# STU's projection by disjoint column segments, each with its own sum of mixed matrices, in a fused convolution, attention and STU kernel

## Chip, cores and metric

The kernel runs on one core of a Trainium2 chip. The metric is the device time of one execution in microseconds (us). Before the change it is 6336.3 us, the median of three runs (6332.32 to 6337.62). The profile is of one further execution, with a span of 6345.8 us and a mean granted TensorE clock of 0.921 of full speed.

## What is computed

The reference has two layers on x of shape (4 images, 48, 48, 128), all in fp32. The first is a two-dimensional selective scan (four directions, 256 channels, 16 states) with a depthwise convolution ahead of it and a gate and a projection behind it. The second works on 2304 tokens an image: softmax attention of the normalised tokens with themselves, and then an STU (spectral transform unit), which is the part that the change touches:

```python
def _stu(u, sigma, phi, Mu, Mpp, Mpm):
    # U_plus:  16 causal convolutions of u with the filters phi[:, k]
    # U_minus: the same of u * (-1)^t, times (-1)^t
    out  = einsum('btkd,k,kde->bte', U_plus,  sigma ** 0.25, Mpp)
    out += einsum('btkd,k,kde->bte', U_minus, sigma ** 0.25, Mpm)
    for i in range(3):                       # the three-tap part
        out += einsum('btd,de->bte', shifted(u, i), Mu[i])
    return out

for i, frac in enumerate((1, 2, 4, 8)):      # four "experts" on shorter and shorter heads
    xi = x[:, :T // frac]
    outs.append(zero_padded(_stu(xi, sigma, phi, M_u[i], M_phi_plus[i], M_phi_minus[i])))
out = sum(outs[i] * weights[i])
```

Every convolution is causal, so its value at a token doesn't depend on where the sequence is cut. All four experts therefore need the same convolutions and differ only in the matrices behind them and in how many tokens they cover: all 2304, the first 1152, the first 576 and the first 288. A token among the first 288 needs the weighted sum of four matrices, one among the last 1152 that of a single one.

## The kernel before

**Stages.** The program is written in a fixed order for each engine[...]. For each image there is a stage of scans (24 chunks of 384 positions, 8 units each, so 192 units) and a stage of attention, in which the next image's prologue is interleaved. TensorE's spare time in the scans takes other work: in image 0's scans the mixing of the STU matrices (`mixture`), in the scans of images 1 to 3 the STU of the image before (`stu`). The STU of image 3 runs alone at the end. `scans` deals this work out by columns: after each quarter of a unit, `more` draws pieces of it until its share of the total columns is done. The totals are `MIX_COLS` and `STU_COLS`, beside `CHUNK_COLS` = 6144 columns a chunk for the scans' own matmuls.

**STU.** Tokens are laid out in four phases of 576 positions, and positions in five blocks (`BLOCKS`), of 128, 128, 128, 128 and 64 positions. An item is a block and one of the 16 filters, 80 items an image. For each item six convolutions (`conv`, L990) multiply Toeplitz tiles `tt`, loaded by overlapping rows from `fd`, with the stationary tokens; ScalarE and VectorE combine them into `U` (eight groups of the block's positions). `project` (L1056) then multiplies U with two matrices a sign, and sums over the 16 filters in one PSUM bank. It runs one item late: after the third convolution of the next item. `ar` (L1046) opens the bank with the three-tap part. `fetch` (L960) keeps four `tt` buffers filled, `fetch_G` (L971) loads the item's mixed matrices `G` into one of two buffers right after the item's first convolution, and `begin` (L1029) loads those of the three-tap part, `mue`, once a block. All these loads go through the SyncE queue.

**Which matrix where.** The four experts end at positions 576, 288, 144 and 72 of a phase. So block 0 changes its sum at 72, block 1 at 16 columns (144 - 128), block 2 at 32 (288 - 256), and blocks 3 and 4 don't change. The fourth entry of `BLOCKS`, `extra`, is that column. Before, the matmuls overlap: the sum of the experts that reach over the whole block is applied to all of its w columns, and the matrix of the one expert that ends inside it to its first `extra` columns, added in PSUM. The scratch tensors `gd` and `mud` hold six matrices each for this, and the third entry, `place`, says where the pair of the block begins.

**Mixing.** `mixture` runs over the 16 filters k. It loads `M` (four experts, two signs; L829) through the SyncE queue, lets ScalarE build diagonal matrices `W` (L833, L834), and multiplies (L847): for each sign q one PSUM tile (j = 1) with running sums, made by broadcasting one expert's matrix over several slots, and one (j = 0) with single matrices. `keep_` copies a tile to SBUF on ScalarE (L822), one group late, and after the second tile stores the pair to `gd` through the SyncE queue (L824). `weights` does the same for the three-tap matrices, on VectorE, in the first image's prologue.

Of the kernel before, what the change touches and what calls it, by code (L numbers as in the profile page):

```python
# [8 lines left out]
F32 = mybir.dt.float32  # L9
AF = mybir.ActivationFunctionType  # L10
ALU = mybir.AluOpType
# [4 lines left out]
P = 128  # L16
B, H, W, C = 4, 48, 48, 128
# [8 lines left out]
KF = 16  # L26
NF = 4
# [6 lines left out]
SLOT = 2 * (LF + 1)  # L34


BLOCKS = [(0, 128, 0, 72), (128, 256, 2, 16), (256, 384, 4, 32), (384, 512, 5, 0), (512, 576, 5, 0)]
SHIFT = 55.0


# [14 lines left out]
def hybrid_kernel(ctx: ExitStack, tc: tile.TileContext, a: dict, out: bass.AP):  # L55
# [3 lines left out]
    nc = tc.nc  # L59
# [3 lines left out]
    res = ctx.enter_context(tc.tile_pool(name="res", bufs=1, space=DRAM))  # L63
# [72 lines left out]
    zs = res.tile([NH, P, L], F32, name="zd")  # L136
    td = res.tile([L, C], F32, name="td")
    ud = res.tile([P, 4, 1 + LF], F32, name="ud")
    gd = res.tile([KF, P, 2, 2 * NF - 2, C], F32, name="gd")
    mud = res.tile([P, 2 * NF - 2, 3, C], F32, name="mud")  # L140
    fd = res.tile([KF, 3, 2, LF + P], F32, name="fd")
    xdd = [[res.tile([P, CS], F32, name=f"xdd{k}_{c}") for c in range(L // CS)] for k in range(2)]

# [597 lines left out]

    MIX_COLS = KF * 2 * 2 * (6 + 3) * C

    ws = wp.tile([P, KF, NF], F32, name="ws")

    def weights(one):

        def load(name, shape, src):
            t = one.tile(shape, F32, name=name)
            nc.scalar.dma_start(t, src)
            return t

        lg = load("lg", [P, NF], a["log_weights"].partition_broadcast(P))
        gu = load("gu", [P, NF], a["gumbel"].partition_broadcast(P))
        sg = load("sg", [P, KF], a["sigma"].partition_broadcast(P))
        ph = load("ph", [KF, 2, 2, LF + P + 1], a["phi"])  # L760
        mu = load("mu", [P, NF, 3, C], a["M_u"].rearrange("i j d e -> d i j e"))
        for i in range(6):
            yield
        hard, wts = [one.tile([P, NF], F32, name=n) for n in ("hard", "wts")]
        m = one.tile([P, 2], F32, name="m")

        nc.vector.tensor_add(lg, lg, gu)
        nc.vector.tensor_reduce(m[:, 0:1], lg, AX.X, ALU.max)
        nc.vector.tensor_scalar(lg, lg, m[:, 0:1], None, ALU.subtract)
        nc.scalar.activation(lg, lg, AF.Exp)  # L770
        yield

        fc = one.tile([KF, 3, 2, LF + P], F32, name="fc")
        n = LF + P
        nc.vector.tensor_copy(fc[:, 0], ph[:, :, 0, :n])
        yield
        nc.vector.tensor_sub(fc[:, 1], ph[:, :, 1, 1:], ph[:, :, 0, :n])
        yield
        nc.vector.tensor_sub(fc[:, 2], ph[:, :, 1, :n], ph[:, :, 0, :n])
        nc.scalar.dma_start(fd, fc)  # L780
        yield
        nc.vector.tensor_reduce(m[:, 0:1], lg, AX.X, ALU.add)
        nc.vector.reciprocal(m[:, 0:1], m[:, 0:1])
        nc.vector.tensor_scalar_mul(lg, lg, m[:, 0:1])
        nc.vector.tensor_reduce(m[:, 0:1], lg, AX.X, ALU.max)
        nc.vector.tensor_scalar(hard, lg, m[:, 0:1], None, ALU.is_equal)
        nc.vector.memset(m[:, 1:2], 1.0)
        yield
        for i in range(NF):

            nc.vector.tensor_tensor(hard[:, i:i + 1], hard[:, i:i + 1], m[:, 1:2], ALU.mult)
            nc.vector.tensor_tensor(m[:, 1:2], m[:, 1:2], hard[:, i:i + 1], ALU.subtract)
        nc.vector.tensor_sub(wts, hard, lg)
        nc.vector.tensor_add(wts, wts, lg)
        yield

        quarter = one.tile([P, KF], F32, name="quarter")
        nc.vector.memset(quarter, 0.25)
        nc.gpsimd.tensor_tensor(sg, sg, quarter, ALU.pow)
        mum = one.tile([P, 2 * NF - 2, 3, C], F32, name="mum")  # L800
        nc.vector.tensor_scalar_mul(mum[:, 5], mu[:, 0], wts[:, 0:1])
        for i in range(1, NF):
            nc.vector.tensor_scalar_mul(mum[:, 6 - 2 * i], mu[:, i], wts[:, i:i + 1])
            if i < NF - 1:
                nc.vector.tensor_tensor(mum[:, 5 - 2 * i], mum[:, 7 - 2 * i], mum[:, 6 - 2 * i], ALU.add)
            yield
        nc.scalar.dma_start(mud, mum)
        for i in range(NF):
            nc.vector.tensor_scalar_mul(ws[:, :, i], sg, wts[:, i:i + 1])
        zero = one.tile([P, 4, 1], F32, name="zero")  # L810
        nc.vector.memset(zero, 0.0)
        nc.scalar.dma_start(ud[:, :, 0:1], zero)

    def mixture(pool, ps):

        late = []
        banks = [0]

        def keep_(G, p, j, k, q):
            nc.scalar.copy(G[:, :, j], p)  # L822
            if j == 0:
                nc.sync.dma_start(gd[k, :, q], G.rearrange("p s j c -> p (s j) c"))  # L824

        for k in range(KF):
            M = [pool.two.tile([P, NF, C], F32, tag=f"M{j}", name=f"M{j}_{k}") for j in range(2)]
            for t, src in zip(M, ("M_phi_plus", "M_phi_minus")):
                nc.sync.dma_start(t, a[src][:, k].rearrange("i d e -> d i e"))  # L829

            W = pool.two.tile([P, 2, NF, P], F32, tag="W", name=f"W{k}")
            for i in range(NF):
                nc.scalar.activation(W[:, 0, i], ident, AF.Copy, scale=ws[:, k, i:i + 1])  # L833
                nc.scalar.activation(W[:, 1, i], nident, AF.Copy, scale=ws[:, k, i:i + 1])  # L834
            yield 0
            for q in range(2):
                G = pool.two.tile([P, 3, 2, C], F32, tag="Gm", name=f"Gm{k}_{q}")
                for j in (1, 0):
                    p = ps.psc.tile([P, 3, C], F32, tag=("c", "q0", "q1")[banks[0] % 3], name=f"G{k}_{q}_{j}")
                    banks[0] += 1  # L840
                    for i in range(NF):

                        n = NF - 1 - i if j else 1
                        if i == (NF - 1 if j else 0):
                            continue
                        for t in range(2):
                            nc.tensor.matmul(p[:, :n] if j else p[:, NF - 1 - i], W[:, q if t else 0, i],  # L847
                                             M[t][:, i].unsqueeze(1).to_broadcast([P, n, C]) if j else M[t][:, i],
                                             start=(t == 0 and (i == 0 or not j)),
                                             stop=(t == 1 and (i == NF - 2 or not j)))  # L850
                            yield n * C
                    if late:
                        keep_(*late.pop())
                    late.append((G, p, j, k, q))
        keep_(*late.pop())

    def begin_stu(b):
# [6 lines left out]
    def tail(b, J, T, po, pool, ps):  # L864
# [38 lines left out]
        for j in range(4):  # L903
# [5 lines left out]
        nc.sync.dma_start(ud[:, :, 1 + P * J:1 + P * J + k], uT.rearrange("c (j p) -> c j p", j=4))  # L909

    STU_COLS = sum(KF * 12 * sum(hi - max(lo, J * P) for J in range((hi + P - 1) // P))
                   + (2 * KF + 3) * 4 * (hi - lo + extra) + 4 * (hi - lo) for lo, hi, place, extra in BLOCKS)

    def stu(b, pool, ps):

# [15 lines left out]
        tts, Gs, Q, U, now, nxt = {}, {}, {}, {}, {}, [0]  # L931
        late = []
        banks = {}
# [98 lines left out]

        def parts(w, extra):

            return ((w, 1), (extra, 0)) if extra else ((w, 0),)

        def ar(n):

            (lo, hi, place, extra), k = items[n]
            w = hi - lo  # L1040
            p = ps.psp.tile([P, 512], F32, tag="p", name=f"pr{b}_{n}")
            now["p"] = p = p[:, :4 * w].rearrange("p (f r m) -> p f r m", f=2, r=2)
            for i, (v, x) in enumerate(parts(w, extra)):
                for j in range(3):
                    src = now["x"][:, 2 - j:6 - j].rearrange("p (r f) m -> p f r m", f=2)
                    nc.tensor.matmul(p[:, :, :, :v], now["mu"][:, x, j, :], src[:, :, :, :v],  # L1046
                                     start=(i == 0 and j == 0), stop=False)
            yield 3 * 4 * (w + extra)

        def project(n):  # L1050
            (lo, hi, place, extra), k = items[n]
            w = hi - lo
            p = now["p"].rearrange("p f r m -> p (f r) m")
            for q in range(2):
                for v, x in reversed(parts(w, extra)):
                    nc.tensor.matmul(p[:, :, :v], Gs[n][:, q, x, :], U[n][:, 4 * q:4 * q + 4, :v], start=False,  # L1056
                                     stop=(k == KF - 1 and q == 1 and v == w))
                yield 4 * (w + extra)
            if k == KF - 1:
                late.append(lambda: kept(n, now["p"], w))  # L1060

# [83 lines left out]
    for b in range(B):  # L1145
        sp = Stage(tc, f"h{b}", "left", s=(6, SB))
        ps = Stage(tc, f"b{b}", "right", psa=(1, PSUM), psy=(1, PSUM), psB=(1, PSUM), psc=(1, PSUM), psp=(1, PSUM))
# [106 lines left out]
```

## Time and profile before

The stages below are stretches of the trace; "busy" is in us. A busy TensorE says that matmuls stood one after another, not that each ran at its peak. Projection is L1056, three taps L1046.

| stretch (us) | what | span | TensorE busy | VectorE busy | projection busy | three taps busy |
|---|---|---|---|---|---|---|
| 112 to 1115 | scans of image 0, mixing | 1003 | 603.1 | 897.3 | none | none |
| 1394 to 2540 | scans of image 1, STU of 0 | 1146 | 1055.6 | 977.1 | 173.4 | 16.5 |
| 2814 to 3960 | scans of image 2, STU of 1 | 1146 | 1056.3 | 976.8 | 173.4 | 15.2 |
| 4234 to 5380 | scans of image 3, STU of 2 | 1146 | 1058.6 | 982.8 | 174.5 | 15.2 |
| 5635 to 6346 | STU of image 3 alone | 711 | 698.8 | 67.1 | 166.5 | 16.9 |

The stretches between them hold attention and the prologues. The row of a kind of instruction gives its count in the whole program and the mean of one; in the trace each fp32 matmul of the program is two passes, so 1024 matmuls of the projection are the 2048 passes counted there, 512 in each image. A mean over passes of several widths says little by itself; the widths have to be taken apart.

### The profile page before, as it was taken

What the parts mean: (1) busy time and instruction counts of PE and PEld (TensorE: products, weight loads), DVE (VectorE), ACT (ScalarE), POOL (GpSimd) and SP (SyncE); (2) the same over time, 40 slices, a digit from 0 to 9 for tenths busy, and PEclk for the clock granted to TensorE, in tenths of its full rate; (3) what the DMA queues carried; (4) which work ended last, traced back from release to release, by engine and by line L of the source; (5) the groups of instructions that cost most, each with busy time, mean ns of one, the idle gap of its engine ahead of it and who ended that gap; (6) DMA issues with size and microseconds to landing.
All of it is one profiled execution on the core that took longest, in us unless ns stands there. A gap on an engine that the chain in (4) does not pass through costs nothing.

```text
span 6345.8 us, 76244 instructions
## 1 busy us (share of the span) xinstructions
PE 5413.9 (85%) x25032; PEld 3360.4 (53%) x25032; DVE 4482.4 (71%) x5562; ACT 3050.9 (48%) x6461; POOL 3637.0 (57%) x1825
## 2 busy tenths in 40 slices
PE   3665666788999998788999998789999998889999
PEld 1222222444555666534556667534555666557889
DVE  6998899458888997458889987458899987211000
ACT  2666666245555654245556654246566654222111
POOL 1888888306787886207778886207778877100000
PEclk6777787799999999899999999889999999899999
DMA  4656655127788888127788888127888887025446
GB/s 105 145 139 150 154 144 143 35 64 180 193 213 218 228 220 237 40 63 188 194 208 223 226 229 223 37 71 189 197 213 221 226 224 222 20 74 153 149 142 214
DMA packets 658251, 1033.57 MB, mean 163 GB/s; under 512 B 93856, under 2 KB 515872, under 8 KB 633120
## 3 DMA queue, kind: packets, MB, share of 16 engines
q1 hardware_dynamic: 652032, 1025.00, 62.7%
q10 hardware_dynamic: 5824, 3.69, 0.3%
q8 instruction: 200, 3.28, 0.2%
q14 instruction: 195, 1.60, 0.1%
HBM read 905.79 MB, written 122.56 MB: 162 GB/s over the span
## 4 chain that ended last, share of the span: by engine, by line
PE 50%; DMA 19%; DVE 18%; ACT 4%; SPq 3%; issue 3%; POOL 3%; DVEq 0%; ACTq 0%; POOLq 0%
PE cv L990 23%; DMA tt<-fd 8%; DVE s L467 7%; PE pr L1056 7%; DMA rep<-dtdud 6%; PE y L484 4%; DVE s L457 4%; PE s L726 3%; PE o L719 3%; DMA bc<-xdd 2%; PE B L448 2%; PE op L662 2%; DVE xc L266 2%; DMA G<-gd 2%; POOL s L476 2%
## 5 line engine op out<-in xcount | busy, mean ns | idle before, releaser
L467 DVE TENSOR_TENSOR_SCAN s<-dA,s 128x385 f32<-128x385 f32 x3072 | 2760.2, 942 | 382.8 <-ACT dA L464 379.6
L476 POOL TENSOR_TENSOR s<-s,bc 128x1536 f32<-128x1536 f32 x768 | 2439.0, 3177 | 200.7 <-DVE s L467 104.3
L464 ACT ACTIVATE dA<-rep,A 128x384 f32<-128x384 f32 x3072 | 1781.9, 585 | 1259.9 <-DVE s L467 1219.1
L990 PE MATMUL cv<-tt,u 128*128 128x256 f32 (+3 forms) x7680 | 1650.8, 354 | 129.2 <-DMA tt<-fd 65.5
L990 PEld LDWEIGHTS cv<-tt,u 128*128 128x128 f32 x7680 | 1271.9, 193 | 649.1 <-issue 303.9
L457 POOL TENSOR_TENSOR s<-rep,bc 128x1536 f32<-128x1536 f32 x288 | 994.0, 3451 | 92.9 <-DMA bc<-xdd 92.9
L457 DVE TENSOR_TENSOR s<-rep,B 128x1536 f32<-128x1536 f32 x480 | 832.8, 1735 | 83.3 <-PE B L448 54.1
L990 PE MATMUL cv<-tt,us 128*128 128x256 f32 (+3 forms) x3840 | 855.2, 352 | 37.2 <-DMA tt<-fd 31.3
L484 PE MATMUL y<-s,csum 128*32 128x384 f32 x6144 | 717.3, 542 | 115.1 <-DVE ya L490 78.8
L990 PEld LDWEIGHTS cv<-tt,us 128*128 128x128 f32 x3840 | 640.7, 192 | 231.5 <-issue 64.7
L1019 DVE TENSOR_TENSOR U<-cv,Q 128x256 f32<-128x256 f32 (+1 forms) x640 | 244.5, 382 | 705.5 <-PE cv L990 696.9
L1056 PE MATMUL pr<-U,G 128*128 128x512 f32 (+4 forms) x2048 | 693.2, 468 | 2.1 <-ACT U L1016 2.1
L448 PE MATMUL B<-xd,spread 128*128 128x384 f32 x960 | 440.1, 543 | 175.5 <-DVE s L457 166.7
L1016 ACT COPY U<-cv 128x256 f32<-128x256 f32 (+1 forms) x640 | 223.0, 349 | 700.9 <-PE cv L990 700.3
L475 POOL COPY carry<-s 128x4 f32<-128x4 f32 x640 | 120.7, 189 | 691.3 <-DVE s L467 660.0
L1056 PEld LDWEIGHTS pr<-U,G 128*128 128x128 f32 x2048 | 335.8, 190 | 193.6 <-issue 140.7
L1004 ACT COPY Q<-cv 128x256 f32<-128x256 f32 (+3 forms) x640 | 223.0, 349 | 385.2 <-PE cv L990 381.7
L726 PE MATMUL s<-xnT 128*128 128x512 f32 (+1 forms) x720 | 357.7, 582 | 42.6 <-ACT xnT L688 23.4
L728 ACT ACTIVATE e<-s,shift 128x512 f32<-128x512 f32 (+1 forms) x360 | 231.0, 644 | 314.1 <-PE s L726 313.5
L484 PEld LDWEIGHTS y<-s,csum 128*32 128x32 f32 x6144 | 127.1, 112 | 467.0 <-issue 314.0
L160 POOL TENSOR_TENSOR ln_vu<-ln_vu,mhalf 128x4 f32<-128x4 f32 (+1 forms) x20 | 26.8, 1340 | 601.9 <-DVE ln_vu L159 601.9
L719 PE MATMUL o<-e,xn 128*128 128x512 f32 (+1 forms) x720 | 343.2, 560 | 4.5 <-ACT e L728 4.5
(161 smaller groups left out, 3761.9 us busy)
## 6 DMA issues: line engine op xcount, KB each, us to landing
rep<-dtdud SPq DMA_DIRECT2D x768, 384.0 KB, 7.7
tt<-fd SPq DMA_DIRECT2D x192, 577.0 KB, 5.3
bc<-xdd SPq DMA_DIRECT2D x2304, 48.0 KB, 3.5
tt<-fd SPq DMA_DIRECT2D x192, 513.0 KB, 4.6
tt<-fd SPq DMA_DIRECT2D x192, 385.0 KB, 4.3
dtdud<-re SPq DMA_DIRECT2D x768, 96.0 KB, 2.3
G<-gd SPq DMA_DIRECT2D x192, 256.0 KB, 5.6
tt<-fd SPq DMA_DIRECT2D x64, 514.0 KB, 5.9
```

The costliest lines, as they stand in the source:

```text
L448: nc.tensor.matmul(self.bt[:, :CS], spread[:, self.ch.k // 2, self.q].rearrange("p c j -> p (c j)"), self.ch.xd, start=True, stop=True)
L457: eng.tensor_tensor(s, self.ch.rep[self.h][:, 1], bt.unsqueeze(1).to_broadcast([P, G4, CS]), ALU.mult)
L464: nc.scalar.activation(dA[:, 1:CS + 1], ch.rep[self.h][:, 0, g], AF.Exp, scale=A[:, ch.k, self.h * G4 + g, self.q:self.q + 1])
L467: nc.vector.tensor_tensor_scan(s, dA[:, CS + 1:0:-1] if ch.rev else dA[:, :CS + 1], s, 0.0, ALU.mult, ALU.add)
L476: nc.gpsimd.tensor_tensor(self.s, self.s, ch.bc[Q4 + self.q].unsqueeze(1).to_broadcast([P, G4, CS]), ALU.mult)
L484: nc.tensor.matmul(ch.y[g * DL:(g + 1) * DL, :CS], csum, self.s[:, g], start=(self.q == 0), stop=(self.q == Q4 - 1))
L719: nc.tensor.matmul(po[J][:, :w], xn[:, i], e[:, :w], start=(i == 0), stop=(i == NT - 1))
L726: nc.tensor.matmul(p[:, :w], xnT[:, i * P:(i + 1) * P], xnT[:, 512 * J:512 * J + w], start=True, stop=True)
L728: nc.scalar.activation(e[:, :w], p[:, :w], AF.Exp, bias=shift)
L990: nc.tensor.matmul(p2[:, :, at - first:], x, t[:, :, hi - 1 - at + J * P:end if end >= 0 else None:-1], start=(c < 2 and J == 0), stop=(J ...
L1019: nc.vector.tensor_tensor(dst, src, q, ALU.add)
L1056: nc.tensor.matmul(p[:, :, :v], Gs[n][:, q, x, :], U[n][:, 4 * q:4 * q + 4, :v], start=False, stop=(k == KF - 1 and q == 1 and v == w))
```

## The change

The segments are made disjoint. The first `extra` columns of a block get one matmul with the full sum that holds there, the other w - `extra` columns one matmul with the sum that holds behind. Then a column is multiplied once, not twice, and four sums (all four experts, three, two, one) take the place of six matrices in `gd` and `mud`: block 0 uses sums 0 and 1, block 1 sums 1 and 2, block 2 sums 2 and 3, blocks 3 and 4 sum 3. The mixing makes the four sums in one PSUM tile a sign instead of two tiles of three, with one copy and one store. The start flag of the bank stays with the first matmul alone, although that one now covers the first segment only.

The diff, without the changes of the tensors' sizes (six slots to four in `gd`, `mud` and `mum`):

```diff
-BLOCKS = [(0, 128, 0, 72), (128, 256, 2, 16), (256, 384, 4, 32), (384, 512, 5, 0), (512, 576, 5, 0)]
+BLOCKS = [(0, 128, 0, 72), (128, 256, 1, 16), (256, 384, 2, 32), (384, 512, 3, 0), (512, 576, 3, 0)]
...
-    MIX_COLS = KF * 2 * 2 * (6 + 3) * C
+    MIX_COLS = KF * 2 * NF * (NF + 1) * C
...
-            nc.vector.tensor_scalar_mul(mum[:, 6 - 2 * i], mu[:, i], wts[:, i:i + 1])
-            if i < NF - 1:
-                nc.vector.tensor_tensor(mum[:, 5 - 2 * i], mum[:, 7 - 2 * i], mum[:, 6 - 2 * i], ALU.add)
+            nc.vector.tensor_scalar_mul(mum[:, NF - 1 - i], mu[:, i], wts[:, i:i + 1])
+            nc.vector.tensor_tensor(mum[:, NF - 1 - i], mum[:, NF - 1 - i], mum[:, NF - i], ALU.add)
...
-        def keep_(G, p, j, k, q):
-            nc.scalar.copy(G[:, :, j], p)
-            if j == 0:
-                nc.sync.dma_start(gd[k, :, q], G.rearrange("p s j c -> p (s j) c"))
+        def keep_(p, k, q):
+            G = pool.two.tile([P, NF, C], F32, tag="Gm", name=f"Gm{k}_{q}")
+            nc.scalar.copy(G, p)
+            nc.sync.dma_start(gd[k, :, q], G)
...
-                G = pool.two.tile([P, 3, 2, C], F32, tag="Gm", name=f"Gm{k}_{q}")
-                for j in (1, 0):
-                    p = ps.psc.tile([P, 3, C], F32, tag=("c", "q0", "q1")[banks[0] % 3], name=f"G{k}_{q}_{j}")
-                    banks[0] += 1
-                    for i in range(NF):
-
-                        n = NF - 1 - i if j else 1
-                        if i == (NF - 1 if j else 0):
-                            continue
-                        for t in range(2):
-                            nc.tensor.matmul(p[:, :n] if j else p[:, NF - 1 - i], W[:, q if t else 0, i],
-                                             M[t][:, i].unsqueeze(1).to_broadcast([P, n, C]) if j else M[t][:, i],
-                                             start=(t == 0 and (i == 0 or not j)),
-                                             stop=(t == 1 and (i == NF - 2 or not j)))
-                            yield n * C
-                    if late:
-                        keep_(*late.pop())
-                    late.append((G, p, j, k, q))
+                p = ps.psc.tile([P, NF, C], F32, tag=("c", "q0", "q1")[banks[0] % 3], name=f"G{k}_{q}")
+                banks[0] += 1
+                for i in range(NF):
+
+                    n = NF - i
+                    for t in range(2):
+                        nc.tensor.matmul(p[:, :n], W[:, q if t else 0, i],
+                                         M[t][:, i].unsqueeze(1).to_broadcast([P, n, C]),
+                                         start=(t == 0 and i == 0), stop=(t == 1 and i == NF - 1))
+                        yield n * C
+                if late:
+                    keep_(*late.pop())
+                late.append((p, k, q))
...
-                   + (2 * KF + 3) * 4 * (hi - lo + extra) + 4 * (hi - lo) for lo, hi, place, extra in BLOCKS)
+                   + (2 * KF + 3) * 4 * (hi - lo) + 4 * (hi - lo) for lo, hi, place, extra in BLOCKS)
...
-            return ((w, 1), (extra, 0)) if extra else ((w, 0),)
+            return ((0, extra, 0), (extra, w, 1)) if extra else ((0, w, 0),)
...
-                    nc.tensor.matmul(p[:, :, :, :v], now["mu"][:, x, j, :], src[:, :, :, :v],
-                                     start=(i == 0 and j == 0), stop=False)
-            yield 3 * 4 * (w + extra)
+                    nc.tensor.matmul(p[:, :, :, v0:v1], now["mu"][:, x, j, :], src[:, :, :, v0:v1],
+                                     start=(j == 0 and v0 == 0), stop=False)
+            yield 3 * 4 * w
...
-                for v, x in reversed(parts(w, extra)):
-                    nc.tensor.matmul(p[:, :, :v], Gs[n][:, q, x, :], U[n][:, 4 * q:4 * q + 4, :v], start=False,
-                                     stop=(k == KF - 1 and q == 1 and v == w))
-                yield 4 * (w + extra)
+                for v0, v1, x in parts(w, extra):
+                    nc.tensor.matmul(p[:, :, v0:v1], Gs[n][:, q, x, :], U[n][:, 4 * q:4 * q + 4, v0:v1], start=False,
+                                     stop=(k == KF - 1 and q == 1 and v1 == w))
+                yield 4 * w
```

More of the change, by code (lines that the diff above doesn't have):

```diff
@@ L138, in hybrid_kernel @@
     ud = res.tile([P, 4, 1 + LF], F32, name="ud")
-    gd = res.tile([KF, P, 2, 2 * NF - 2, C], F32, name="gd")
-    mud = res.tile([P, 2 * NF - 2, 3, C], F32, name="mud")
+    gd = res.tile([KF, P, 2, NF, C], F32, name="gd")
+    mud = res.tile([P, NF, 3, C], F32, name="mud")
     fd = res.tile([KF, 3, 2, LF + P], F32, name="fd")
@@ L799, in weights @@
         nc.gpsimd.tensor_tensor(sg, sg, quarter, ALU.pow)
-        mum = one.tile([P, 2 * NF - 2, 3, C], F32, name="mum")
-        nc.vector.tensor_scalar_mul(mum[:, 5], mu[:, 0], wts[:, 0:1])
+        mum = one.tile([P, NF, 3, C], F32, name="mum")
+        nc.vector.tensor_scalar_mul(mum[:, NF - 1], mu[:, 0], wts[:, 0:1])
         for i in range(1, NF):
-            nc.vector.tensor_scalar_mul(mum[:, 6 - 2 * i], mu[:, i], wts[:, i:i + 1])
-            if i < NF - 1:
-                nc.vector.tensor_tensor(mum[:, 5 - 2 * i], mum[:, 7 - 2 * i], mum[:, 6 - 2 * i], ALU.add)
+            nc.vector.tensor_scalar_mul(mum[:, NF - 1 - i], mu[:, i], wts[:, i:i + 1])
+            nc.vector.tensor_tensor(mum[:, NF - 1 - i], mum[:, NF - 1 - i], mum[:, NF - i], ALU.add)
             yield
@@ L1042, in ar @@
             now["p"] = p = p[:, :4 * w].rearrange("p (f r m) -> p f r m", f=2, r=2)
-            for i, (v, x) in enumerate(parts(w, extra)):
+            for v0, v1, x in parts(w, extra):
                 for j in range(3):
                     src = now["x"][:, 2 - j:6 - j].rearrange("p (r f) m -> p f r m", f=2)
-                    nc.tensor.matmul(p[:, :, :, :v], now["mu"][:, x, j, :], src[:, :, :, :v],
-                                     start=(i == 0 and j == 0), stop=False)
-            yield 3 * 4 * (w + extra)
+                    nc.tensor.matmul(p[:, :, :, v0:v1], now["mu"][:, x, j, :], src[:, :, :, v0:v1],
+                                     start=(j == 0 and v0 == 0), stop=False)
+            yield 3 * 4 * w
         def project(n):
@@ L1054, in project @@
             for q in range(2):
-                for v, x in reversed(parts(w, extra)):
-                    nc.tensor.matmul(p[:, :, :v], Gs[n][:, q, x, :], U[n][:, 4 * q:4 * q + 4, :v], start=False,
-                                     stop=(k == KF - 1 and q == 1 and v == w))
-                yield 4 * (w + extra)
+                for v0, v1, x in parts(w, extra):
+                    nc.tensor.matmul(p[:, :, v0:v1], Gs[n][:, q, x, :], U[n][:, 4 * q:4 * q + 4, v0:v1], start=False,
+                                     stop=(k == KF - 1 and q == 1 and v1 == w))
+                yield 4 * w
             if k == KF - 1:
```

## The prediction

> **What bounds the kernel now.** I read the busy row and the slices first, then a table of stages, then the chain of waits inside the last stage, because one average over 6346 us hides that TensorE has three different roles.
>
> ```profile
> PE 5413.9 (85%) x25032; PEld 3360.4 (53%) x25032; DVE 4482.4 (71%) x5562; ACT 3050.9 (48%) x6461; POOL 3637.0 (57%) x1825
> ...
> PE   3665666788999998788999998789999998889999
> ...
> DMA  4656655127788888127788888127888887025446
> ```
>
> TensorE is the busiest engine, but its slices run from 5-6 (first scans) to 9 (scans with STU, and the end). The table of stretches (span; busy time of TensorE, weight loads, VectorE, ScalarE, GpSimd; granted clock, DMA share, GB/s) separates the first scans (the matrices are mixed there), the scans of image 1 with STU of image 0, and STU of the last image alone:
>
> ```profile
> 112.00:1115.00 1003.00, 603.12 (x2606) 244.47 (x2607) 897.33 (x961) 608.59 (x1250) 850.00 (x416) 0.77 0.61 147
> ...
> 1394.00:2540.00 1146.00, 1055.59 (x5311) 667.29 (x5310) 977.09 (x1151) 648.17 (x1405) 866.78 (x421) 0.97 0.83 210
> ...
> 5635.00:6346.00 711.00, 698.82 (x3460) 568.28 (x3460) 67.09 (x165) 115.14 (x325) 0.00 (x0) 0.99 0.55 161
> ```
>
> The end is pure TensorE: 12 us idle of 711. The scans with STU are mostly TensorE (92%), with VectorE at 85% and DMA at 0.83 close behind; images 2 and 3 look the same (1056 and 1059 us busy of 1146). The first scans are VectorE and GpSimd; TensorE has 40% to spare. In the end stage the chain of waits (start, us, work, number of passes) gives the price of one filter's projection, in block 0, 1 and 2:
>
> ```profile
> 5698.47 2.61 PE cv L990 x12
> 5701.08 2.69 PE pr L1056 x8
> ...
> 5739.86 3.19 PE pr L1046 x12
> ...
> 5745.70 2.16 PE pr L1056 x8
> 5747.87 5.19 PE cv L990 x24
> ...
> 5880.90 2.16 PE pr L1056 x8
> 5883.07 7.78 PE cv L990 x36
> ```
>
> The convolution's 256-column passes take 7.78/36 = 216 ns, so 0.833 ns a column with almost nothing fixed; each program matmul is two passes. In block 0 eight passes are four of 512 and four of 288 columns: 4 x 427 + 4 x 240 = 2.67 us, against 2.69 shown. In blocks 1 and 2 four passes of 512 leave 2.16 - 1.71 = 0.45 us for four narrow ones: 113 ns each, for 64 as for 128 columns. So a narrow pass has a floor of 113 ns and a wide one is paid by column.
>
> [...] I use the trace's 0.833 ns per pass and column. [...]
>
> **The change part by part.**
> *Projection (L1056), 48 of 80 items an image.* Instructions stay at four a filter. The wide matmul shrinks: 512 to 224 columns in block 0, 448 in block 1, 384 in block 2; all stay above the floor (187, 373, 320 ns). Saved per filter, four passes each: 4 x 288 x 0.833 = 0.96, 4 x 64 x 0.833 = 0.21, 4 x 128 x 0.833 = 0.43 us. Sum 1.60, times 16 filters: 25.6 us an image.
> *The three-tap part (L1046).* Six wide passes a block lose the same columns: 6 x 480 x 0.833 = 2.4 us an image; somewhat more for block 0 of the last image, whose clock is still low there. Together **28 us of TensorE an image**. Strided column ranges cost nothing extra: the 288-column passes are such ranges already.
> *G and mue loads (L971, L1029).* The same bytes and runs: two neighbouring matrices, or one. Zero, as nothing changes.
> *STU_COLS.* Work is dealt to the scan units by columns, 24 x 6144 + 406,944 = 554,400 before, 16,800 fewer after (-3.0%): the saving is spread over the whole stage.
> *End stage.* All on the path: -28 us. One wait may appear. G of the next item is issued 0.6 us after an item starts and used one item and 1.3 us later. An item of block 0 falls from 5.30 to 4.33 us, so the lead from 6.0 to 5.0 us, and these loads land in 4.7 to 5.1 us (median 5.0). Nothing to 0.4 us a filter is lost, 0 to 6 us; I take 3. **-25 us.**
> *Scans with STU.* The share of the 28 us that shortens the stage is not measured, so I bound it. In the first 706 us of the stage of image 1 (blocks 0 to 2) L1056 is busy 128.8 us, and the chain's shares there (10.3, 13.2, 8.9, 8.3% of stretches of 126, 140, 200, 240 us) put 69 us of it on the path: 54%, and over all three stages 54, 48 and 46%. The upper bound is all of it. I take 0.6, near the lower end: DMA needs grow. The scans move about 123 MB a stage (107 GB/s); block 0 adds 16 x 0.66 MB in 9.6% of the columns, 110 us, 203 GB/s in all; after, in 8.0%, 90 us, 226 GB/s, where the best slice of the page reaches 237. **-17 us a stage, -51 us for three**; both ends: -14 and -28 a stage.
> *Mixing (L847), in the first scans.* Per filter and sign 12 matmuls of 2304 columns become 8 of 2560: 256 columns x 2 passes x 0.833 x 32 = +14 us of TensorE (18 at its clock of 0.77), where 400 us are idle. ScalarE: 64 copies of 471 ns become 32 of some 0.6 us (582 ns for the 512-column copy of L1064): -11 us where 394 us are idle. Stores fall from 32 x 384 KB to 32 x 256 KB, of 0.61 share. All beside other work: zero.
> *A wait moved.* The SyncE queue is in order, and its store of mixed matrices waits for ScalarE's copy. The next filter's matrices M are queued behind it, and TensorE, which has the scans' spreads and sums queued behind the mixing matmul, waits for M:
>
> ```profile
> SPq L824 <- ACT Gm L822: 194.1, 30, 10.5
> ```
> ```profile
> PE G L847 <- DMA M<-in_M_phi_plus: 75.2, 12, 17.0
> ```
> ```profile
> 404.07 0.34 SPq L824 DMA_DIRECT2D gd<-Gm  x1
> 404.50 1.81 SPq L435 DMA_DIRECT2D bc<-xdd  x4
> 406.40 1.76 SPq L408 DMA_DIRECT2D rep<-dtdud  x4
> 408.26 0.40 SPq L829 DMA_DIRECT2D M<-in_M_phi_plus  x1
> ```
>
> In the program order of after, that store stands directly ahead of M; before, 5 to 20 other issues stand between. M then starts about 1 us after ScalarE's copy, the one just ahead of its W activations; in this trace that copy starts between 0.5 us before and 5.9 us after M's issue (412.08 against 408.26 in the stretch shown), so M would be issued 49 us later, summed over 15 filters. Against this: where four rep loads go out just ahead of M, nine filters, M lands in about 9.0 us, elsewhere in 3.4. In the order of after the rep loads are on their way before the store waits, so M should land in 3.4 there too: issued 40 us later, landing 9 x 5.6 = 50 us faster. The other six lose 9 us. Net about nothing: I take **zero for the stage**, ends -15 and +25 us (all 49 us later, half on the path as now, where M has 4.0% of the stage's chain, 40 us, of 78 us waited).
> *Weights and start.* One more VectorE add of 384 columns and a smaller store, in a prologue with 33 us of VectorE idle of 112: below 1 us, zero.
> Sum: -25 - 51 + 0 = -76; 6336.3 - 76 = **6260 us**.
>
> **The rivals.**
> *All TensorE time comes back:* -28 in four stages, -112 to -113, 6223 us. For it: 92 to 98% busy; direct waits of TensorE for tt in the stage of image 1 are only 36 us. Against: half of the chain lies elsewhere.
> *Transfers hold the scans:* only the end gains, -25, 6311 us. For it: DMA share 0.83 and 27% of the chain of that stage on DMA (tt 13.8, rep 8.7, bc 2.7, G 2.5). Against: TensorE idles only 90 us of 1146.
> *The mixing pays (slower):* M is issued 49 us later in sum, lands no faster, all of it is on the path, with 18 us of extra matmul, and the scans gain nothing: +67 - 25 = +42, 6378 us. For it: the store ahead of M, and spreads and sums queued behind. Against: the landing times above. Half of it, with the same end, comes to about +8, inside what can be told from no change.
>
> **How the numbers follow.** The partial gain 53%, all of it 20%, the end alone 18%, slower 6%, about equal 3%. The range runs from the second case to the third, 6222 to 6311; it leaves out the last two and the outer edges of those two. Faster 0.91, same 0.03, slower 0.06.
>
> **What would show it.** End stage: an item of block 0 at 4.3 to 4.7 us (5.30), block 1 at 7.1, block 2 at 9.5; L1056 busy some 26 us less; a wait of L1056 for G, if any, below 6 us. Scan stages 1126 to 1132 us with TensorE near 1028 busy; had they stayed at 1146 with more tt and rep waits, the second rival is right. First scans 988 to 1028 us, M landing in 3 to 5 us everywhere, and TensorE's waits for M near 75 us. I would be wrong by mechanism if narrow passes cost more than 113 ns or the wide ones don't follow their columns.

## The result, and the profile after

The changed kernel takes 6302.85 us (median of four runs, 6296.46 to 6311.58), against 6336.64 us before in the same comparison. The ratio is 0.9949, with a 95% interval of 0.9932 to 0.9966: faster by 0.5%, some 32 us. The forecast was 76 us. The direction and the range (6222 to 6311) held, the size did not: less than half of it came.

The same lines of the page, after:

```profile
PE 5345.6 (85%) x24776; PEld 3339.5 (53%) x24776; DVE 4482.0 (71%) x5563; ACT 3039.2 (48%) x6429; POOL 3639.1 (58%) x1825
...
PE   3666666797999998888999998888999998889999
...
DMA  4556555127888888128888888128888888026546
```

TensorE is busy for 68 us less in all; the span of this profiled run (6309.8 us) is 36 us less. The shares look the same, so the page alone doesn't tell where the rest went. The table of stretches does (columns as before: span, busy time of TensorE, weight loads, VectorE, ScalarE, GpSimd; clock, DMA share, GB/s). First scans, scans of image 1, end stage:

```profile
124.00:1142.00 1018.00, 623.52 (x2396) 211.40 (x2396) 912.73 (x977) 609.84 (x1237) 872.80 (x423) 0.77 0.58 140
1445.00:2550.00 1105.00, 1021.09 (x5344) 668.34 (x5344) 972.77 (x1142) 640.29 (x1402) 873.45 (x422) 0.97 0.84 214
...
5624.00:6310.00 686.00, 672.50 (x3460) 568.24 (x3460) 67.14 (x165) 115.33 (x325) 0.00 (x0) 0.99 0.57 167
```

From the start of its first VectorE scan (L467) to the start of its last, each stage went as follows, in us:

| stage | before | after | difference | forecast |
|---|---|---|---|---|
| first scans, mixing | 1012.8 | 1017.9 | +5.1 | 0 |
| scans of image 1 | 1117.4 | 1105.1 | -12.3 | -17 |
| scans of image 2 | 1118.0 | 1117.0 | -1.0 | -17 |
| scans of image 3 | 1111.5 | 1107.4 | -4.1 | -17 |
| behind the last scan (end stage with the last attention) | 955.5 | 930.9 | -24.6 | -25 |

The end came as forecast. The three scan stages gave 17 us in place of 51.

In the end stage the chain of waits shows the new prices, in block 0, 1 and 2:

```profile
5664.19 1.73 PE pr L1050 x8
5665.92 2.61 PE cv L984 x12
5668.53 0.02 issue
5668.55 1.97 PE pr L1050 x8
...
5734.74 1.95 PE pr L1050 x8
5736.69 5.19 PE cv L984 x24
...
5860.70 1.74 PE pr L1050 x8
5862.44 7.78 PE cv L984 x36
```

The projection of a filter falls from 2.69, 2.16 and 2.16 us to 1.73, 1.95 and 1.74, where the working gave 1.71, 1.95 and 1.73. In block 0 about every second filter takes 1.97 us instead; the experiment on G below shows why. L1050 (L1056 before) is busy 141.6 us there, 25.0 less.

In the scans, the place to look is how long each block takes. The three-tap passes of a block stand right behind its first item's convolutions, so the start of the first of them marks the block. A stretch from mark to mark holds 15 items of its block and the first of the next. In the timeline of the stage of image 1, before and after:

```profile
1449.12 0.67 PE L1046 MATMUL pr<-ux,mue 128*128 128x512 f32 x1 [2.48 <-DMA mue<-mud]
...
1603.99 0.59 PE L1046 MATMUL pr<-ux,mue 128*128 128x512 f32 x1
...
1807.48 0.59 PE L1046 MATMUL pr<-ux,mue 128*128 128x512 f32 x1
...
2070.34 0.59 PE L1046 MATMUL pr<-ux,mue 128*128 128x512 f32 x1
...
2356.97 0.63 PE L1046 MATMUL pr<-ux,mue 128*128 128x256 f32 x1
```
```profile
1455.44 0.82 PE L1040 MATMUL pr<-ux,mue 128*128 128x288 f32 x1 [2.71 <-DMA mue<-mud]
...
1586.51 0.67 PE L1040 MATMUL pr<-ux,mue 128*128 128x64 f32 x5
...
1795.70 0.61 PE L1040 MATMUL pr<-ux,mue 128*128 128x128 f32 x4
...
2051.02 0.59 PE L1040 MATMUL pr<-ux,mue 128*128 128x512 f32 x1
...
2344.92 0.60 PE L1040 MATMUL pr<-ux,mue 128*128 128x256 f32 x2
```

Block 0 took 154.9 us before (1603.99 - 1449.12) and takes 131.1 after. Block 3, whose matmuls the change doesn't touch, took 286.6 and takes 293.9. That is the riddle: a block whose own work is the same takes 7 us longer.

### The profile page after: what moved, and what is told of

Its sections match the earlier page's. It is cut to its first block, busy times and chain, and to the rows that moved or that the text cites. A ratio compares the mean times of both kernels' runs of the same rounds, so it can differ in the third digit from the quotient of the medians.

```text
span 6309.8 us, 75729 instructions
## 1 busy us (share of the span) xinstructions
PE 5345.6 (85%) x24776; PEld 3339.5 (53%) x24776; DVE 4482.0 (71%) x5563; ACT 3039.2 (48%) x6429; POOL 3639.1 (58%) x1825
## 4 chain that ended last, share of the span: by engine, by line
PE 46%; DVE 20%; DMA 18%; ACT 5%; issue 4%; SPq 3%; POOL 3%; DVEq 0%; ACTq 0%; POOLq 0%
PE cv L984 21%; DVE s L467 8%; DMA tt<-fd 7%; PE pr L1050 5%; DVE s L457 4%; PE y L484 4%; PE s L726 3%; DMA rep<-dtdud 3%; DMA G<-gd 3%; PE o L719 3%; DMA bc<-xdd 3%; PE op L662 2%; PE B L448 2%; POOL s L476 2%; DVE xc L266 2%
## 5 line engine op out<-in xcount | busy, mean ns | idle before, releaser
L467 DVE TENSOR_TENSOR_SCAN s<-dA,s 128x385 f32<-128x385 f32 x3072 | 2761.5, 944 | 335.9 <-ACT dA L464 334.5
L1050 PE MATMUL pr<-U,G 128*128 128x288 f32 (+7 forms) x2048 | 596.1, 422 | 11.0 <-DMA G<-gd 9.3
L448 PE MATMUL B<-xd,spread 128*128 128x384 f32 x960 | 443.7, 547 | 182.6 <-DVE s L457 170.6
L1050 PEld LDWEIGHTS pr<-U,G 128*128 128x128 f32 x2048 | 339.9, 192 | 158.6 <-issue 81.5
```

The costliest lines, as they stand in the source:

```text
L448: nc.tensor.matmul(self.bt[:, :CS], spread[:, self.ch.k // 2, self.q].rearrange("p c j -> p (c j)"), self.ch.xd, start=True, stop=True)
L467: nc.vector.tensor_tensor_scan(s, dA[:, CS + 1:0:-1] if ch.rev else dA[:, :CS + 1], s, 0.0, ALU.mult, ALU.add)
L1050: nc.tensor.matmul(p[:, :, v0:v1], Gs[n][:, q, x, :], U[n][:, 4 * q:4 * q + 4, v0:v1], start=False, stop=(k == KF - 1 and q == 1 and v1 == w))
```

## The experiments

Times are compared by the ratio to runs of the kernel before on the same chip, since its median moved between 6336 and 6347 us from one comparison to the next. Stages are from each kernel's profiled run, one execution each.

**The segments alone** (e1_stu_alone), in the kernel before:

```diff
-            return ((w, 1), (extra, 0)) if extra else ((w, 0),)
+            return ((0, extra, 0), (extra, w, 1)) if extra else ((0, w, 0),)
...
-                yield 4 * (w + extra)
+                yield 4 * w
```

> The disjoint segments alone, in the kernel before: projection and three taps by segments and STU_COLS smaller, but mixing, stores and the six slots as before. (The first segment of a block is then multiplied by the single expert's matrix, not by the full sum[...].) Theory A, the parts are independent: the first scans go back to 1013 us from their first to their last VectorE scan (1018 in the changed kernel), the end stage keeps its 25 us, the scans with STU keep their small gain of about 6 us each: 6296 to 6300 us. Rival B, the mixing change or the smaller tensors in memory hold the later stages back: the scans with STU gain the 17 us each of the forecast here, 6260 to 6270 us.

Measured: 6295.2 us, ratio 0.9929 (0.9916 to 0.9941). The first scans take 1014.3 us, the scans with STU 1105.1, 1108.1 and 1107.9, the part behind the last scan 927.6. So the missing gain isn't in the mixing: the scan stages are 8.6 us shorter than before on average, nowhere near the 17 of rival B. With the single expert's matrix in the first segment the part behind the last scan is within 3.3 us of the changed kernel's (930.9).

**A larger dose** (e2_half_projection): half of the projection left out of the changed kernel.

```diff
-            for q in range(2):
+            for q in range(1):
```

> The changed kernel with the projection of one of the two signs left out (half of its matmuls; all loads, convolutions and evacuations stay, and STU_COLS is less by that half). It is a second, larger dose of the same medicine: 71 us of TensorE less in each STU. End stage in every theory: about 71 us less. Theory A, TensorE sets the pace of the scans with STU at the share of 0.6 of the forecast: 43 us less in each, 6303 - 71 - 128 = 6104 us. Theory B, the share seen for the first dose, 0.2: 14 us each, 6190 us. Theory C, the scans' own chain on VectorE, ScalarE and GpSimd sets the pace and TensorE time is worth nothing there: 6232 us.

Measured: 6211.5 us, ratio 0.9797 (0.9783 to 0.9810). The scan stages (1097.7, 1090.6, 1093.7) are 15.8 us shorter each on average than in the changed kernel. The 71 us of the expectation are half of L1050's busy time; by the prices in the chain of waits (1.73, 1.95, 1.74, 1.72 and 0.87 us a filter in the five blocks) half of the projection is 64 us. So the scan stages give back 0.25 of it. The end fell by 55.9: block 0 there loses only 8.6 us of the 13.7 us of matmul taken from it, because loads of G now hold it (half of its chain of waits, 14% in the changed kernel). The total lies between theories B and C, and the scan stages are close to B's 14 us. But that is not what TensorE time is worth, as the next two show: here too `STU_COLS` fell, and block 0's share of it (34,816 of 353,280 columns, 18.9 units).

**The old dealing** (e4_old_pace): the changed kernel with the old counts in `yield` and `STU_COLS`. Not one instruction is added or left out; only the order in which STU's work is mixed into the scans differs.

```diff
-            yield 3 * 4 * w
+            yield 3 * 4 * (w + extra)
...
-                yield 4 * w
+                yield 4 * (w + extra)
```

> The changed kernel, but STU's work is dealt to the scan units by the columns of before (the overlapping ones counted twice), so that blocks 0 to 2 are spread over as many units as before while their matmuls are shorter. Theory A, the smaller counts packed the short items of blocks 0 to 2, with their fixed loads and evacuations, more densely into the scans, and that took the gain back: 8 to 11 us less in each scan stage, 6270 to 6280 us. Rival B, the scans' own chain or the transfers at the end of the stage set the pace whatever the dealing is: within 5 us of the changed kernel, 6298 to 6308 us.

Measured: 6278.6 us, ratio 0.9902 (0.9886 to 0.9917), 24 us below the changed kernel (30 by the ratios), as theory A has it. The scan stages take 1103.3, 1103.4 and 1093.2.

**The new dealing with the old matmuls** (e12_new_pace_old_columns), in the kernel before:

> The kernel before, every matmul as it was, but STU's work dealt by the counts of the changed kernel (w in place of w + extra; STU_COLS to match). With before, e1_stu_alone and e4_old_pace it makes a table of two by two, columns of TensorE against dealing. Theory A, the new dealing alone costs what the shorter matmuls bring: some 7 to 11 us more in each scan stage than before, 6358 to 6375 us, block 0 faster, blocks 1, 3 and 4 slower. Rival B, the dealing matters only together with the shorter matmuls: 6330 to 6345 us.

Measured: 6378.9 us, ratio 1.0048 (1.0034 to 1.0062): slower than before, by 0.5%, with block 0 faster and blocks 1, 3 and 4 slower, as theory A has it. (The median lies above theory A's range, but before is slower in this comparison too, at 6347 us.) The stretch of image 1's scans in e4, in e12 and in the kernel before:

```profile
1446.00:2550.00 1104.00, 1016.70 (x5344) 665.12 (x5344) 973.28 (x1143) 641.61 (x1402) 874.04 (x422) 0.98 0.84 215
```
```profile
1440.00:2564.00 1124.00, 1040.54 (x5344) 663.96 (x5344) 972.63 (x1141) 640.73 (x1402) 873.30 (x422) 0.98 0.84 210
```
```profile
1439.00:2556.00 1117.00, 1040.97 (x5344) 664.34 (x5344) 973.52 (x1142) 641.80 (x1402) 873.03 (x422) 0.98 0.83 212
```

All have the same 5344 passes and the same granted clock. The last two have the same matmuls, and TensorE is busy for the same time within 0.5 us; the dealing alone makes the stretch 7 us longer. e4 and e12 differ in both, columns and dealing: TensorE's busy time by 24 us and the spans by 20. Together with before and after this is a table of two by two (mean of the three scan stages, us):

| | old dealing | new dealing | dealing costs |
|---|---|---|---|
| old columns | 1115.6 (before) | 1124.5 (e12) | +8.9 |
| new columns | 1099.9 (e4) | 1109.8 (after) | +9.9 |
| columns bring | -15.7 | -14.7 | |

The two effects add up. The shorter matmuls bring 15 us a stage, 0.53 to 0.56 of the 28 us of TensorE that the prediction counted; the new counts take 9 to 10 back. These are single profiles: other kernels with the same columns and dealing (e1 and e7; e11) lie within about 3 us of the means here, and the three stages of one kernel differ among themselves (the dealing costs between 2 and 14 us in a single one). The times of whole executions agree on the sum: from old to new dealing the ratio rises by 0.0048 (before to e12), 0.0047 (e4 to after) and 0.0044 (e11 to e7), 28 to 30 us in three stages.

The blocks show how (means of the three stages, in us). A block's share of the units is its part of STU's columns times 192; counted are the VectorE scans between its mark and the next, four a unit. The counts differ from the shares because a stretch begins behind its block's first item:

| | block 0 | block 1 | block 2 | block 3 | block 4 |
|---|---|---|---|---|---|
| units by share, old dealing | 25.0 | 32.9 | 45.6 | 55.1 | 33.3 |
| units by share, new dealing | 21.2 | 33.3 | 45.4 | 57.4 | 34.8 |
| units counted, before | 25.8 | 34.5 | 46.2 | 53.2 | 30.8 |
| units counted, e12 and after | 21.8 | 35.5 | 45.5 | 55.5 | 32.2 |
| before | 154.9 | 204.3 | 260.7 | 286.7 | 199.6 |
| e12 (new dealing) | 140.7 | 212.0 | 260.4 | 294.2 | 207.6 |
| e4 (new columns) | 145.9 | 202.0 | 255.4 | 287.9 | 198.9 |
| after (both) | 131.0 | 211.0 | 257.7 | 293.9 | 206.8 |

The new dealing moves 4 scan units out of block 0, one into block 1 and the rest into blocks 3 and 4. Block 0 gets rid of 14.2 us for them (before to e12), 3.6 us a unit, while the other blocks grow by 22.9 us in all, 5.7 us for each unit that they receive. From e4 to after it is 3.9 and 6.3. The difference is what the dealing costs. Block 1's one unit more costs 7.7 us, not far above the 5.9 us that a unit takes there on average; blocks 3 and 4 grow by 15.5 us. A likely reason why block 0 frees so little is that its 16 items keep their loads, convolutions and evacuations; the experiments below test parts of this.

**Sparser still** (e6_sparser): w + 3 extra.

> The changed kernel, dealt by w + 3 extra columns in place of w (e4_old_pace: w + extra), which spreads block 0 over 16.1% of the units (11.0% in the changed kernel, 13.0% in e4_old_pace) and takes them from the other blocks. Theory A, the fixed loads and evacuations of the short items are what costs in the scans: lower again than e4_old_pace, 6262 to 6274 us. Rival B, it is a matter of balance, and what is taken from blocks 3 and 4 (transfers of the largest tiles) is given back there: 6279 us or more.

Measured: 6378.6 us, ratio 1.0053 (1.0038 to 1.0067). Rival B is right. Block 0, with 31.9 units by share (16.6%, not the 16.1% expected), takes 186.5 us: it pays 40.6 us more than in e4 for 7.7 more units counted. The other blocks lose as many and get only 7.7 us shorter together; block 4, with 30.8 in place of 33.3 units, still takes 199.3. So a unit costs much where it goes and frees little where it is taken, in this direction too. It is a balance, and of the three dealings tried the old one is the best.

**G half an item earlier** (e5_g_half_item_earlier):

```diff
-                if i == 0:
-                    fetch_G(n)
+                if i == 3:
+                    fetch_G(n + 1)
```

> The changed kernel, with G of the next item requested after the fourth convolution of an item in place of after the first one of its own: half an item earlier, in the same two buffers. Theory A, G comes late for the shortened items: the end stage loses the 4 us by which it missed its computed 28, and each scan stage several us more: 6275 to 6290 us. Rival B, G's waits only stand where others would: the end stage alone, 6297 to 6303 us.

Measured: 6312.6 us, ratio 0.9955 (0.9941 to 0.9969), not to be told from the changed kernel, and somewhat above both expectations. Block 0 of the end falls from 79.7 to 76.8 us, in its steady part every filter's projection takes 1.73 us, none 1.97, and G is gone from its chain of waits. So the wait for G that was put at 3 us is there. The scans don't gain (mean 1110.7, after 1109.8). A whole item earlier (e3_g_earlier) gave no time: it needs four buffers of G, and that pool then takes 26.1 KB a partition where 23.6 KB are left.

**Which fixed work of an item costs?** Three kernels with the new dealing take one part each away: G loaded once a block (e9_g_once_a_block); Q and VectorE's sum left out of the evacuation (e10_no_vector_sums); the tile of block 0 loaded once (e13_tt_once_block0). The edit of the first:

```diff
+                if k:
+                    Gs[n] = Gs[n - 1]
+                    return
```

> The changed kernel, with G loaded for the first filter of a block alone and used for all 16 (so the filters' matrices are not the right ones; every matmul has its shape and count). It takes 75 of 80 G loads an image away, 256 or 128 KB each, some 15 MB of about 240 MB a stage. Theory A, the loads of the items, dealt more densely, take TensorE's gain back in the scans: each scan stage falls by 10 us or more and the end stage by 4: below 6270 us. Rival B, it is not the loads but the evacuations and the scans' own chain: the scans stay within 4 us each, 6287 to 6300 us.

Measured: 6270.1 us, ratio 0.9887 (0.9872 to 0.9902). The scan stages fall by 10.0 us on average and the end by 4.1, just at theory A's edge. But of this block 0, the dense one, gives only 3.1; most of the rest comes from blocks 2 and 4 (3.2 and 2.9).

> The changed kernel with VectorE out of STU's evacuation: the copy Q of the shared convolution and the sum with it are left out, and ScalarE copies in place of the sum (four ScalarE copies an item as before, VectorE's two sums an item of 0.4 us gone, some 60 us a stage; U lacks the shared term). Theory A, what an item costs a scan unit beside its columns is its evacuation on VectorE: blocks 0 and 1, which have the most items a unit, fall most, 10 us or more each, the scan stages 20 us or more each: below 6250 us. Rival B, it is the loads: within 5 us a stage, 6288 to 6305 us.

Measured: 6286.6 us, ratio 0.9900 (0.9884 to 0.9917). The scan stages fall by 9.4 us; blocks 0 and 1 by 3.9 and 5.1. Neither theory fits the stages, though the total lies just below rival B's range.

> The changed kernel with the Toeplitz tile of block 0 loaded for the first filter alone and used for all 16 (so block 0 convolves with the wrong filters): 15 loads of 387 KB an image less, all in block 0. Theory A, loads limit block 0 in the scans: block 0 falls by 8 us or more from 131 us. Rival B, the evacuations and the scans' own chain limit it: within 4 us of 131 us. End stage the same in both.

Measured: 6288.1 us, ratio 0.9902 (0.9882 to 0.9923). Block 0 in the scans falls by 3.7 us, within rival B's bound; in the end stage it falls too (79.7 to 75.0 us), which neither expected. Each part is worth 3 to 4 us of block 0; none of them is the cause by itself. None was tried with the old dealing, so these runs don't say how much of the dealing's cost each part carries.

**M a filter ahead** (e7_m_ahead), in the mixing:

```diff
+            M = ahead.pop(k) if k else fetch_M(0)
+            if k + 1 < KF:
+                ahead[k + 1] = fetch_M(k + 1)
```

> The changed kernel, with the matrices M of the next filter loaded a whole filter ahead in the mixing (same two buffers), so that neither the store nor ScalarE's copy stands between. Theory A, half of TensorE's 91 us of waits for M is on the path of the first scans: they fall from 1018 to about 975 us, 6260 us in all. Rival B, TensorE has 40% to spare there and its other waits (for VectorE's products and sums) take over: the 5 us that the change cost this stage come back and little more, 6293 to 6300 us.

Measured: 6273.9 us, ratio 0.9892 (0.9878 to 0.9907). The first scans take 984.3 us, 33.6 less, nearer to theory A's 975 than to rival B. TensorE's waits for M, in the list of waits of the changed kernel and then of this one (total, times, longest):

```profile
PE G L842 <- DMA M<-in_M_phi_plus: 91.2, 14, 17.3
```
```profile
PE G L850 <- DMA M<-in_M_phi_plus: 17.2, 1, 17.2
```

74 us of waits are gone, and 0.45 of them come back as time. This is worth as much as the whole change, in a stage where TensorE is busy for 61%: in the program's order the scans' spreads and sums stand behind the mixing matmul that waits, and stop with it. In the changed kernel's timeline TensorE starts nothing from 417.56 to 421.63 us, 4.08 of them put down to M; then the mixing matmul runs, and the next spread (L448) starts at 423.47.

**Both repairs** (e11_pace_and_m):

> The changed kernel with both repairs: the dealing of before (as e4_old_pace) and M loaded a filter ahead (as e7_m_ahead). If the two are independent, as they lie in different stages: 6302.9 - 24.2 - 29.0 = 6250 us, 1.4% below before. If one eats the other: above 6265 us.

Measured: 6254.4 us, ratio 0.9848 (0.9832 to 0.9865), faster than before by 1.5% and than the changed kernel by 1%. The two repairs add up: together they lower the ratio by 0.0101, apart by 0.0047 and 0.0057. This version beats both kernels.

**Old counts for block 0 alone** (e14_pace_block0_and_m):

> As e11_pace_and_m, but the old counts (w + extra) are kept for block 0 alone; blocks 1 and 2 are dealt by w. Block 0 gets 13.3% of the units (11.0% in the changed kernel, 13.0% in e11_pace_and_m), blocks 3 and 4 together 46.8% (48.0 and 46.0%). Theory A, the density of block 0 is the whole story of the dealing: the same as e11_pace_and_m within 8 us, 6246 to 6262 us. Rival B, what costs is every unit moved to blocks 3 and 4: between the two dealings, 10 us or more above e11_pace_and_m, 6264 us or more.

Measured: 6272.7 us, ratio 0.9889 (0.9872 to 0.9907), by which rival B is right: by the ratios it is some 26 us above e11, and the two intervals lie clear of each other. But its six runs spread from 6252 to 6279, and the profiled one is the second fastest of them (span 6258.9 us, scan stages 1103.9 on average against 1103.0 in e11), so it doesn't show where the others lose time. The density of block 0 is not the whole story; what the rest is stays open.

## Why the prediction was half right

*The prices.* A wide pass by its columns, a narrow one at 113 ns, strided segments at no extra cost: right to 0.02 us (1.73, 1.95, 1.74 us), where no wait for G is added. The weight loads of the end stage stayed as they were: 3460 loads in 568.28 us before, 568.24 after, beside a TensorE that idles for 12 of 711 us and 13.5 of 686. The three-tap part of block 0 of the last image fell from 5.97 to 4.38 us on the chain of waits, by 1.59 where the prices give 1.44; the granted clock was 0.72 in that stretch before (5646 to 5652 us) and 0.63 after (5635 to 5639.5), and 1.00 right behind it in both. That the second segment needs no zeroing was an assumption; the trace of before doesn't show it. The changed kernel spends no instruction on it: the projection has 2048 passes as before, and VectorE in all one instruction more (5563), the add in the prologue.

*The end stage, -25 us.* Right: -24.6; the same end in e4, e7 and e11 gives -24 to -28. G's wait in block 0 was put at 3 us, the middle of a range of 0 to 6, and taking it away gave 2.9. That both meet so closely is partly luck.

*The share of 0.6 in the scans, -17 us a stage.* Nearly right when the dealing doesn't move: -15.7 and -14.7, in the two columns of the table of two by two. It was a choice between bounds, and the share of L1056 on the chain of waits before (46 to 54%) was as good a guide.

*"Work is dealt to the scan units by columns ... the saving is spread over the whole stage": this is the step that failed.* It gave the dealing no cost of its own; that block 0 gets denser it used only to choose the share. A smaller count not only spreads a saving, it moves scan units from the block whose count fell most to those whose count didn't fall. That costs 9 to 10 us a stage, some 28 us in three, and it is most of the some 40 us between forecast and result; the mixing (5 us) and the 2 us a stage by which 0.6 was too high make up the rest. Beside it stands a slip: block 0's 53,088 columns were divided by 554,400, which includes the scans' own, and this gave 9.6% and 110 us. Against STU's 406,944 it is 13.0%, 25 units, and the trace of before has 154.9 us for it. The estimate of the transfers there, 203 GB/s before and 226 after, is too high with it: in block 0 of image 1 the traces have 184 and 196. Done for all blocks and for both kernels, the shares of units above could have been had before the run.

*Mixing, zero.* Nearly. The stage is 5.1 us longer in this profile, and 1014.9 to 1019.0 us in all the kernels with the new mixing and its place for M, against 1012.8 to 1014.3 in the three with the old, about 4 us on average. The mechanism came as worked out: the store stands right ahead of M (in all 15 filters behind the first, M is issued 0.4 to 0.5 us after it), M starts late, and lands fast, with the rep loads already through. In the SyncE timeline of after:

```profile
408.44 1.76 SPq L408 DMA_DIRECT2D rep<-dtdud  x4
417.66 0.34 SPq L823 DMA_DIRECT2D gd<-Gm  x1
418.09 0.40 SPq L828 DMA_DIRECT2D M<-in_M_phi_plus  x1
```

The four rep loads here land 4.0 to 8.1 us after their issue, all before 418 us; the store goes out after ScalarE's copy (417.05 to 417.63), and M lands in 3.4 us. M's median landing is 3.6 us, 8.4 before. What was a little off is the balance: TensorE's waits for M rose from 75 to 91 us.

*The rivals.* "Transfers hold the scans" named 6311 us and came near the result, but by luck: with either dealing the scans answer to TensorE's columns, with 15 us a stage. Transfers do count (without the loads of G the stages are 10 us shorter), but they don't hold the scans alone. The slower case didn't come.

*What stays open.* Why a unit frees less where it is taken than it costs where it goes, how an item's fixed cost is made up (loads of G, the tile and VectorE's sums each account for a few us), and why e14, with block 0 dealt about as in e11, is slower than e11. The mixing's part of the difference between e1 (0.9929) and the changed kernel (0.9949) is within the intervals.

## What to carry to other kernels

Where background work is dealt to a foreground loop by a count, an edit of the counts is a change of schedule (here 9 to 10 us a stage by itself), and has to be costed as one: list the loop iterations that each phase gets before and after. Test it apart by keeping the old counts with the new instructions. And before counting saved columns, look for loads that are requested where they are needed: asking for M one filter earlier gave as much as the whole change (33.6 us of the first scans, against some 32).

## What the runs showed of the hardware

One thing was not expected: a phase that looks bound by TensorE need not follow TensorE's columns. Block 3 of image 1 has TensorE busy for 277.33 of 285 us before and for 272.59 of 280 us after, 97% both times. Its own matmuls are the same. It holds 2.3 scan units more after, whose matmuls come to some 3 us (an estimate: 768 columns a unit, two passes of 0.833 ns). The block takes 7.3 us longer, and a unit 5.30 us in place of 5.39.

A second limit lies close by. With M ahead, the first scans, which have no STU, take 5.13 us a unit (984.3/192) while TensorE is busy for 62%; VectorE is busy for 93% there (911.07 of 984 us) and in block 3, before and after (264.71 of 285 us, 261.00 of 280). The chain of waits points the same way: in block 3 of the three scan stages the convolutions hold 31 to 44% of it in the kernels with the old dealing (before, e4, e11), and 20 to 29% in those with the new one (e12, after, e1, e5, e7). So the scans' own chain seems about as long as TensorE's there. No experiment shows which part of it counts; it isn't VectorE's load alone, as block 3 still takes 293.5 us without STU's sums on VectorE (e10), against 293.9.
